# A graph layer on one core: zeros through TensorE in the first segment, PSUM operands for x and h, and another order at the end

## The chip, the core and the metric

The kernel runs on one core of one Trainium2 chip. A core has TensorE for matrix products (PE in the profile, its weight loads PEld), VectorE (DVE), ScalarE (ACT), GpSimd (POOL) and SyncE (SP). In this kernel SP issues nearly all plain DMAs and POOL issues the scatters. TensorE writes to PSUM, 8 banks of 512 fp32 values per partition. The metric is the device time of one launch in microseconds (us), as the median of several runs. "Granted clock" is the share of the full TensorE clock that the records show; in this trace it is 1.0 or 0.5 at any moment, and means lie between.

## The reference, cut to what matters

```
h = relu(layernorm(x)) @ W_in2f                 # 12500 nodes x 128
Wij = ssp(f_ij @ W_f1 + b_f1) @ W_f2 + b_f2     # 412500 edges, 20 -> 128 -> 128
Wij = Wij * rcut_ij[:, None]
x_ij = h[idx_j] * Wij                           # idx_j = dst, sorted
agg = segment_sum(x_ij, idx_i)                  # idx_i = src, unsorted
out = ssp(agg @ W_o1 + b_o1) @ W_o2 + b_o2
return x + out                                  # ssp(x) = softplus(x) - log 2
```

The edges come sorted by the node whose h they read, so that reading is local. The node they are summed into is in no order, so the messages have to be moved to their place.

## The kernel before

**Chunks and segments.** The edges are cut into 806 chunks of 512 edges, four chunks to a group. The chunks are split into seven segments of 88, 44, 30, 14, 14, 8 and 4 groups. Every segment has its own table in HBM (`slots`). A chunk's 512 messages are scattered by POOL into the table of its segment, each to a slot in the block of 128 nodes that it belongs to; four scatters of 128 rows to a chunk. When a segment is complete, its table is read back in "units" (`Collect`), and TensorE adds the rows to their nodes with a 0/1 matrix. So segment 1 is collected while the chunks of segment 2 and later ones are worked on, and during the chunks of the first segment there is no collecting at all. The first segment's chunks are 0 to 351; its collecting begins at step 359 (`DELAY` is 7).

**What one chunk takes.** TensorE: the filter layer `z` for a pair of chunks (`hidden`, L691, 20 rows x 512 columns, twice); the second filter layer `v` (`value`, L801, four products of 128 columns); the picking of the rows of h, `picked` (`pick`, L812, four products with a 0/1 matrix `at` that DVE makes at L785); two products for the ranks of the slots, `free` (L766, L733, 392 columns). ScalarE: softplus's parts of a pair (L700, L701, L703), the bias written into `v` (`bias`, L793), and `hg`, the picked rows times the cutoff (`picked`, L822). VectorE: `r` (L709), `top` (L738), `inb` (L714), and the message `o` = v * hg (`message`, L829 and L830). POOL: the four scatters of `o` (L834).

**The order of the work.** The order on every engine is written out by hand in `step(k, units)`, one call for every k: message of chunk k, then the end of the ranks (`top`) begun in the step before, then `keep` for sums that are finished, then `hg` and `v` of chunk k+1, the picking of chunk k+2, `at` of k+3, `r`, `inb`, the comparing of units (`compare`, L886, the 0/1 matrix `to`), ranks, softplus, the filter layer of the pair that begins at k+4, and last the adding of units on TensorE (`add`, L907). Engines take their instructions in this order. `picked` and `v` share three PSUM banks (tag `v`): the bank of `picked` of chunk k+2 comes free when the message of chunk k has been computed. `z` has a pair of banks of its own, free when `r` has read it. `behind` makes the first product of a filter layer, of `v` and of a picking wait also for a scatter eight steps back.

**Collecting.** `keep` copies (first segment, ScalarE, L928) or adds (later ones, VectorE, L930) a finished quad of four blocks from the PSUM bank `acc` to the sums `agg` in SBUF. There is one `acc` bank while chunks run. A planner spreads the units over the steps from the end of a segment up to step `NCH + BEYOND`; after a unit that ends a quad it lets no other unit into that step. The last segments are collected after the last chunk; then the output layer `finish` runs, quad by quad.

**h and x.** `make_h` computes h for a quad of 512 nodes, 25 quads in all, beside the chunks of the first segment (last at 1344 us). It keeps h as the sum of three bf16 parts: the first is a rounding of the PSUM tile `hps`, then `left` = hps - first part (L370), the second part a rounding of `left` (L371), the third `left` minus the second (L373). x is loaded again for the residual, for 14 quads early (`early_homes`, from step 300, bias added by VectorE at L426) and for the other quads after the last chunks (`late_homes`, bias added by POOL). `count_ps` holds 0 to 127 along the free axis in PSUM, for `inb` and `to`.

Of the kernel before, what the change touches and what calls it, by code (L numbers as in the profile page):

```python
# [17 lines left out]
P = 128  # L18
TG = 16
CH = 512  # L20
# [23 lines left out]
def gnn_kernel(  # L44
# [282 lines left out]
    def make_h(q, psum):  # L327

        n = min(QT, NTILE - q * QT)
        xb = early.pop(q, None)  # L330
        if xb is None:
            xb = load_x(q)
            for _ in range(3):
                yield
        st = ln.tile([P, QT, 6], F32, name="st")
        mv = ln.tile([P, QT, 2], F32, name="mv")
        for i in range(n):
            nc.vector.bn_stats(st[:, i, :], xb[:, i, :])
            nc.vector.bn_aggr(mv[:, i, :], st[:, i, :])

        rs = ln.tile([P, QT], F32, name="rs")
        nc.scalar.activation(rs[:, :n], mv[:, :n, 1], AF.Ln, bias=eps)
        nc.scalar.activation(rs[:, :n], rs[:, :n], AF.Exp, scale=-0.5)
        yield

        ve = ln.tile([P, QT], F32, name="ve")
        nc.vector.tensor_scalar(ve[:, :n], mv[:, :n, 1], EPS, -0.5, op0=ALU.add, op1=ALU.mult)
        r2 = ln.tile([P, QT], F32, name="r2")
        nc.vector.tensor_mul(r2[:, :n], rs[:, :n], rs[:, :n])
        nc.vector.tensor_mul(r2[:, :n], r2[:, :n], ve[:, :n])  # L350
        nc.vector.scalar_tensor_tensor(rs[:, :n], r2[:, :n], 1.5, rs[:, :n],
                                       op0=ALU.add, op1=ALU.mult)
        for i in range(n):
            nc.vector.tensor_scalar(xb[:, i, :], xb[:, i, :], mv[:, i, 0:1], rs[:, i:i + 1],
                                    op0=ALU.subtract, op1=ALU.mult)
        yield
        xps = psum.tile([P, QT, P], F32, name="xps", tag="acc")
        for i in range(n):
            nc.tensor.transpose(xps[:, i, :], xb[:, i, :], ident)
        xT = ln.tile([P, QT, P], F32, name="xT")  # L360
        nc.scalar.activation(xT[:, :n, :], xps[:, :n, :], AF.Relu)
        yield
        hps = psum.tile([P, QT, P], F32, name="hps", tag="acc")
        for i in range(n):
            nc.tensor.matmul(hps[:, i, :], xT[:, i, :], win, start=True, stop=True)
        hb = ln.tile([P, QT, 3, P], BF16, name="hb")
        nc.scalar.activation(hb[:, :n, 0, :], hps[:, :n, :], AF.Copy)
        yield
        left = ln.tile([P, QT, P], F32, name="left")
        nc.vector.tensor_sub(left[:, :n, :], hps[:, :n, :], hb[:, :n, 0, :])  # L370
        nc.scalar.activation(hb[:, :n, 1, :], left[:, :n, :], AF.Copy)  # L371
        yield
        nc.vector.tensor_sub(hb[:, :n, 2, :], left[:, :n, :], hb[:, :n, 1, :])  # L373
        for (b, rows), table in zip(tables, h3_t):
            lo = max(0, b - q * QN) // P
            hi = min(n, (b + rows - q * QN) // P)
            if lo < hi:
                r = q * QN + lo * P - b
                nc.sync.dma_start(
                    table[r:r + (hi - lo) * P, :].rearrange("(c p) f -> p c f", p=P),  # L380
                    hb[:, lo:hi, :, :].rearrange("p c k f -> p c (k f)"))
                if b + rows == QN:
                    yield
            if q == NQ - 1:
                for r in range(NTILE * P - b, rows, P):
                    if r >= 0:
                        nc.sync.dma_start(table[r:r + P, :], none)
        nc.sync.dma_start(
            h3[q * QN:q * QN + n * P, :].rearrange("(c p) f -> p c f", p=P),
            hb[:, :n, :, :].rearrange("p c k f -> p c (k f)"))  # L390
        yield
# [28 lines left out]
        for p, cs, rows in pieces:  # L420
            nc.sync.dma_start(xo[:p, cs, :], x[rows, :].rearrange("(c p) f -> p c f", p=p))

    def x_bias(xo, pieces, engine=nc.vector):
        for p, cs, rows in pieces:
            xi = xo[:p, cs, :]
            engine.tensor_add(xi, xi, spread(bo2[:p, :], xi.shape[1]))  # L426

    def finish(t0, n, sT, quad, psum, z, xo=None, bank=("v", 3)):

# [108 lines left out]
    with tc.tile_pool(name="edge", bufs=2) as edge, tc.tile_pool(  # L538
# [8 lines left out]
        free_v = free.rearrange("p (t b) -> p t b", b=NBLK)  # L547


        count_ps = state_ps.tile([P, P], F32, name="count_ps")  # L550

        def clear(seg):

            todo = []

            def put(b, e, low):

                half = seg.tiles(b) * P // 2
                v = seg.views[VIEWS][seg.row(b):seg.row(e), :].rearrange(
                    "(r c) f -> r (c f)", c=half)  # L560
                for q in range(0, 2 * (e - b), P):
                    n = min(P, 2 * (e - b) - q)
                    for r in range(low, half - low, ZN * ZR):
                        w = min(ZN * ZR, half - low - r)
                        todo.append((
                            v[q:q + n, r * RW:(r + w) * RW].rearrange("r (k f) -> r k f", f=ZR * RW),
                            zero[:n, None, :].to_broadcast([n, w // ZR, ZR * RW])))

            full = (NBLK - 1) // BG * BG
            for b, e in ((0, seg.b0), (seg.b0, min(seg.b1, full)), (seg.b1, full)):  # L570
                if b < e:
                    put(b, e, seg.low)

            for b in range(full, NBLK):
                low = seg.low if b < NBLK - 1 else seg.low_last
                half = seg.tiles(b) * P // 2
                n = (half - 2 * low) // ZR
                for r in range(2):
                    r0 = seg.row(b) + r * half + low
                    todo.append((seg.views[VIEWS][r0:r0 + n * ZR, :]  # L580
                                 .rearrange("(q c) f -> q (c f)", c=ZR), zero[:n, :]))
            return todo

        puts = []

# [8 lines left out]
        class Group:  # L594
# [91 lines left out]
            def hidden(self, c):  # L686

                z = psum.tile([P, 2, CH], F32, name="z")
                for k in range(2):
                    rows = slice(32 * (c + k), 32 * (c + k) + RBF)  # L690
                    mm = nc.tensor.matmul(z[:, k, :], wf1[rows, :], self.f[rows, :],  # L691
                                          start=True, stop=True)
                    if k == 0:
                        behind(mm, self.g * NCHUNK + c - LZ, 3)
                self.pair[c] = z
# [110 lines left out]

            def pick(self, c, at, ps):

                near = self.near.pop(c)
                k = self.g * NCHUNK + c - 2  # L810
                for i in range(QT):
                    mm = nc.tensor.matmul(ps[:, i, :], at[:, i * P:(i + 1) * P], near,  # L812
                                          start=i == 0, stop=i == QT - 1, skip_group_check=True)
                    if i == 0:
                        behind(mm, k, 2 + k % 2)
# [118 lines left out]
        groups = {}  # L934
        NEXT = table_of.index(1) - 1
        LG, LW, LR, LZ = 12, 6, 6, 4
        DELAY, BEYOND = 7, 14

        def of(k):
            return groups[k // NCHUNK], k % NCHUNK  # L940
# [52 lines left out]
        def step(k, units=()):  # L993
# [19 lines left out]
                for _ in r:  # L1013
                    pass
            tops.clear()
            for c in owed:
                c.keep()
            owed.clear()
            if has(k + 1):
                g, c = of(k + 1)  # L1020
                hgs[k + 1] = g.picked(c, ps.pop(k + 1))
# [10 lines left out]
            part("blocks", min(k + LR + 1, 2 * k + 3), blocks)  # L1032
            for c, u in units:
                c.compare(u)
            upto = max(made["rank"], min(k + LR, 2 * k + 3))
            ready = [ranks(j) for j in range(made["rank"] + 1, upto + 1)]
            made["rank"] = upto
# [63 lines left out]
                if todo[i - 1][1].ends(todo[i - 1][2]):  # L1101
                    break

        def x_ahead(homes, engine):

            pending = []
            for q, xo in homes:
# [5 lines left out]
                yield  # L1113
                yield
                if len(pending) > 2:
                    x_bias(*pending.pop(0), engine)
            for w in pending:
                yield
                x_bias(*w, engine)

        def as_quad(t):
            return t.rearrange("p (c f) -> p c f", f=P)

        xs = {}
        NX = 14

        def early_homes():
            for q in range(NX):
                if q < 6:
                    yield q, quad.tile([P, QT, P], F32, name="xo", bufs=6)  # L1130
                elif q < 12:
                    yield q, ln.tile([P, QT, P], F32, name="xo", tag=("xb", "xT", "left")[q // 2 - 3],
                                     bufs=2)
                else:
                    t = ln.tile([P, QT, 3, P], BF16, name="xo", tag="hb", bufs=2)
                    yield q, as_quad(t.rearrange("p c k f -> p (c k f)")[:, :2 * CH].bitcast(F32))
# [14 lines left out]
        def rest():  # L1151
# [14 lines left out]
                    yield  # L1166
            yield from ranges(psum)
            late_biases(psum)

        def side():  # L1170

# [11 lines left out]
        with tc.manual_schedule():  # L1183
# [27 lines left out]
            made["rank"] = 0  # L1211
            group(1)
            aside = side()
            x_early = x_ahead(early_homes(), nc.vector)
            x_late = x_ahead(late_homes(), nc.gpsimd)
            for k in range(-3, max(NCH, max(units) + 1)):
                for seg, d in zeros.get(k, ()):
                    seg.clears.append(nc.sync.dma_start(*d).ins.name)
# [122 lines left out]
```

## Time and profile before

| | |
|---|---|
| median of 8 runs | 5287.85 us (5268.48 to 5309.7) |
| the profiled execution, its own time | 5317.66 us |
| its span, first to last instruction | 5315.9 us |
| POOL: scatters L834 | 3224, 3099.0 us busy, 961 ns each |
| PE busy, share of the span | 3715.0 us, 70% |
| DVE, ACT busy | 3139.1 us, 2784.8 us |
| granted clock, 500 to 1000 us and 2500 to 3000 us | 0.66 and 0.83 |

The stages in time: chunk 0 is scattered at 23 us; the collecting of the first segment begins with `acc` sums near 2300 us (first L928 at 2302.9 us); the last scatter is at 5185.1 us; from there to about 5240 us units are loaded and added, and then the output layer runs to the end. Times per chunk are read off POOL, because every chunk has exactly four scatters: the number of L834 in a window divided by four is the number of chunks. "Releaser" is what ended an engine's wait; `remote` means that a semaphore changed for which the profile shows no instruction.

### The profile page before, as it was taken

How to read it: one execution, taken by the hardware profiler on the slowest of the kernel's cores; microseconds unless marked ns; L12 is line 12 of the kernel's file. 1: busy time of each engine (PE TensorE's matmuls, PEld its weight loads, DVE VectorE, ACT ScalarE, POOL GpSimd, SP SyncE). 2: the span in 40 equal slices, each digit the busy share in tenths (PEclk: the TensorE clock that was granted, in tenths of full speed). 3: DMA queues.
4: the chain of work that ended last, by engine and by line, in shares of the span. 5: the costliest groups of instructions: out<-in, count | busy, mean ns of one | idle time of the engine just before them, and what ended most of it. 6: DMA issues, size and time to landing. Idle time of an engine off the chain costs nothing. (4 is left out here: it accounts for less than half of the span.)

```text
span 5315.9 us, 74340 instructions
## 1 busy us (share of the span) xinstructions
PE 3715.0 (70%) x21594; PEld 2847.6 (54%) x21594; DVE 3139.1 (59%) x7101; ACT 2784.8 (52%) x5466; POOL 3136.7 (59%) x3292
## 2 busy tenths in 40 slices
PE   5565655556556555588887787787777777777778
PEld 3344433444334333366666666666666666665657
DVE  5555555555444444566666666566666666666667
ACT  5555555555555545555555555455544454554443
POOL 5666666666666666666665565555555555555552
PEclk7666666666666666688888888888888888888889
DMA  4445444444433334455656555566655665565546
GB/s 144 143 146 152 141 140 147 125 146 126 117 96 97 96 113 135 124 181 177 182 178 210 169 168 170 154 182 191 173 165 157 188 189 150 171 191 156 158 131 194
DMA packets 515221, 820.65 MB, mean 154 GB/s; under 512 B 177188, under 2 KB 312728, under 8 KB 514812
## 3 DMA queue, kind: packets, MB, share of 16 engines
q1 hardware_dynamic: 411212, 602.55, 40.2%
q0 software_dynamic: 103168, 213.15, 12.0%
q8 instruction: 180, 2.95, 0.2%
q14 instruction: 229, 1.88, 0.1%
q10 hardware_dynamic: 432, 0.13, 0.0%
HBM read 419.75 MB, written 395.69 MB: 153 GB/s over the span
## 5 line engine op out<-in xcount | busy, mean ns | idle before, releaser
L834 POOL DMA_INDIRECT slots<-o,slot x3224 | 3099.0, 961 | 2083.1 <-DVE o L830 1192.1
L822 ACT ACTIVATE hg<-picked,rcut 128x128 f32<-128x128 f32 x3224 | 912.3, 365 | 1371.0 <-remote 732.4
L907 PEld LDWEIGHTS acc<-to,m 128*128 128x128 f32 x8152 | 1202.4, 229 | 467.9 <-issue 307.7
L907 PE MATMUL acc<-to,m 128*128 128x128 f32 x8152 | 1296.7, 320 | 196.6 <-issue 99.5
L801 PEld LDWEIGHTS v<-wf,r 128*128 128x128 f32 x6448 | 1084.5, 249 | 446.6 <-issue 302.9
L801 PE MATMUL v<-wf,r 128*128 128x128 f32 x6448 | 1183.0, 338 | 174.3 <-issue 109.1
L830 DVE TENSOR_TENSOR o<-v,hg 128x512 f32<-128x512 f32 x806 | 552.6, 686 | 969.6 <-remote 513.4
L691 PE MATMUL z<-f,wf 20*128 20x512 f32 x1612 | 626.3, 854 | 468.3 <-DVE r L709 270.0
L886 DVE TENSOR_TENSOR to<-count_ps,m 128x640 f32<-128x640 f32 (+3 forms) x793 | 636.3, 826 | 251.6 <-remote 104.0
L738 DVE TENSOR_REDUCE top<-free 128x4 f32<-128x392 f32 x806 | 448.8, 557 | 475.3 <-remote 267.1
L793 ACT ACTIVATE v<-bf 128x512 f32<-128x512 f32 x806 | 486.0, 603 | 449.0 <-DVE o L830 243.9
L812 PE MATMUL picked<-near,at 96*128 96x128 bf16 x3224 | 386.2, 253 | 374.7 <-DVE o L830 259.5
L709 DVE SCALAR_TENSOR_TENSOR r<-z,nbf,a 128x1024 f32<-128x1024 f32 x403 | 514.0, 1275 | 101.3 <-ACT a L703 56.8
L766 PE MATMUL free<-inb,rest_of 128*128 128x392 f16 x806 | 327.8, 407 | 341.1 <-issue 214.5
L700 ACT ACTIVATE a<-z,bf 128x1024 f32<-128x1024 f32 x403 | 445.0, 1104 | 226.5 <-remote 126.2
L812 PEld LDWEIGHTS <-at 96*128 96x128 bf16 x3224 | 308.2, 116 | 432.8 <-issue 408.1
L691 PEld LDWEIGHTS z<-f,wf 20*128 20x128 f32 x1612 | 156.1, 233 | 679.5 <-DVE r L709 362.3
L703 ACT ACTIVATE a<-a,half 128x1024 f32<-128x1024 f32 x403 | 462.7, 1148 | 13.1
L714 DVE TENSOR_TENSOR inb<-count_ps,blk 128x392 f16<-128x392 f32 x806 | 445.5, 553 | 0.0
L701 ACT ACTIVATE a<-a 128x1024 f32<-128x1024 f32 x403 | 425.9, 1057 | 12.8
L733 PE MATMUL free<-inb,after 128*128 128x392 f16 x806 | 330.9, 411 | 7.1 <-DVE inb L714 3.8
L785 DVE TENSOR_SCALAR at<-rel,prow 96x512 bf16<-96x512 bf16 x806 | 283.3, 352 | 0.0
(113 smaller groups left out, 1226.2 us busy)
## 6 DMA issues: line engine op xcount, KB each, us to landing
m<-slots SPq DMA_DIRECT2D x307, 387.0 KB
m<-slots SPq DMA_DIRECT2D x278, 322.5 KB
rel<-rel_d SPq DMA_DIRECT2D x202, 384.0 KB
slots<-o,slot POOLq DMA_INDIRECT x3224
m<-slots SPq DMA_DIRECT2D x193, 258.0 KB
slots<-zero SPq DMA_DIRECT2D x96, 387.0 KB
f<-in_f_t SPq DMA_DIRECT2D x404, 80.0 KB
slots<-zero SPq DMA_DIRECT2D x58, 516.0 KB
```

The lines of the kernel that those rows point to most:

```text
L691: mm = nc.tensor.matmul(z[:, k, :], wf1[rows, :], self.f[rows, :], start=True, stop=True)
L703: nc.scalar.activation(a, a, AF.Ln, bias=half, scale=0.5)
L709: nc.vector.scalar_tensor_tensor(r, z, nbf1, a, op0=ALU.max, op1=ALU.add)
L738: nc.vector.tensor_reduce(self.top[:, c * QT:(c + 1) * QT], free_v, axis=mybir.AxisListType.X, op=ALU.max)
L793: nc.scalar.activation(v, spread(bf12, QT), AF.Copy)
L801: mm = nc.tensor.matmul(v[:, i, :], r[:, i * P:(i + 1) * P], wf2, start=False, stop=True, skip_group_check=True)
L812: mm = nc.tensor.matmul(ps[:, i, :], at[:, i * P:(i + 1) * P], near, start=i == 0, stop=i == QT - 1, skip_group_check=True)
L822: nc.scalar.activation(hg[:, i, :], ps[:, i, :], AF.Copy, scale=self.rcut[:, j:j + 1])
L830: nc.vector.tensor_mul(o[:, :, :P], v, hg)
L834: put = nc.gpsimd.indirect_dma_start(out=views[j % VIEWS], out_offset=bass.IndirectOffsetOnAxis(ap=self.slot[:, j:j + 1], axis=0), in_=o[: ...
L886: nc.vector.tensor_tensor(to[:, :n, :], count_ps[:, None, :].to_broadcast([P, n, P]), m[:, :n, P:].to_broadcast([P, n, P]), op=ALU.is_equal)
L907: nc.tensor.matmul(self.acc[b // QT][:, i, :], m[:, j, :P], to[:, j, :], start=t == 0, stop=t == self.seg.tiles(b) - 1)
```

## The change

There are four parts.

1. In the steps of the first segment (chunks 8 to 358) TensorE multiplies zeros: 12 products of 384 columns into the bank of `z` in front of each pair's filter layer, and 6 into the bank of `picked` in front of each picking. The results are overwritten by the products that follow. These are 4218 products, and as many weight loads.
2. `keep` moves in `step`, but only in the steps after the last chunk (k >= `NCH`) that have units: there a finished quad is added after the first `compare` of the step and no longer before it. In all other steps, so while chunks run, it stays where it was.
3. PSUM operands: `left` is gone, the differences are formed in the PSUM tile `hps` itself. The bias bo2 is copied to PSUM beside `count_ps`, and the early bias addition of x reads it there. With the room that this frees, two more quads of x are loaded early (16, before 14) and two fewer at the end.
4. `BEYOND`, the number of steps after the last chunk over which the planner may spread units, is 8 (before 14).

```diff
-        left = ln.tile([P, QT, P], F32, name="left")
-        nc.vector.tensor_sub(left[:, :n, :], hps[:, :n, :], hb[:, :n, 0, :])
-        nc.scalar.activation(hb[:, :n, 1, :], left[:, :n, :], AF.Copy)
+        nc.vector.tensor_sub(hps[:, :n, :], hps[:, :n, :], hb[:, :n, 0, :])
+        nc.scalar.activation(hb[:, :n, 1, :], hps[:, :n, :], AF.Copy)
         yield
-        nc.vector.tensor_sub(hb[:, :n, 2, :], left[:, :n, :], hb[:, :n, 1, :])
+        nc.vector.tensor_sub(hb[:, :n, 2, :], hps[:, :n, :], hb[:, :n, 1, :])
...
-    def x_bias(xo, pieces, engine=nc.vector):
+    def x_bias(xo, pieces, engine=nc.vector, b=bo2):
...
-        count_ps = state_ps.tile([P, P], F32, name="count_ps")
+        numbers = state_ps.tile([P, CH], F32, name="numbers")
+        count_ps, bo2_ps = numbers[:, :P], numbers[:, P:2 * P]
...
+        def idle(bank, n):
+
+            for _ in range(n):
+                nc.tensor.matmul(bank[:, :3 * P], none[:, :P], none, start=True, stop=True,
+                                 skip_group_check=True)
...
                 z = psum.tile([P, 2, CH], F32, name="z")
+                if 8 <= self.g * NCHUNK + c < segs[1].c0 + DELAY:
+                    idle(z[:, 0, :], 12)
                 for k in range(2):
...
             def pick(self, c, at, ps):
 
+                if 8 <= self.g * NCHUNK + c < segs[1].c0 + DELAY:
+                    idle(ps.rearrange("p t f -> p (t f)"), 6)
                 near = self.near.pop(c)
...
-        DELAY, BEYOND = 7, 14
+        DELAY, BEYOND = 7, 8
...
-            for c in owed:
-                c.keep()
-            owed.clear()
+            def keep():
+                for c in owed:
+                    c.keep()
+                owed.clear()
+
+            if k < NCH or not units:
+                keep()
...
             for c, u in units:
                 c.compare(u)
+                keep()
...
-        NX = 14
+        NX = 16
...
             late_biases(psum)
+            nc.scalar.activation(bo2_ps, bo2, AF.Copy)
...
-            x_early = x_ahead(early_homes(), nc.vector)
-            x_late = x_ahead(late_homes(), nc.gpsimd)
+            x_early = x_ahead(early_homes(), nc.vector, bo2_ps)
+            x_late = x_ahead(late_homes(), nc.gpsimd, bo2)
```

`none` is a bf16 tile of zeros that both kernels have, for rows of the tables that no node owns.

## The prediction

> **What bounds the kernel now.** I read the page first: busy shares, the 40 slices, and the costliest group.
>
> ```profile
> span 5315.9 us, 74340 instructions
> PE   5565655556556555588887787787777777777778
> POOL 5666666666666666666665565555555555555552
> PEclk7666666666666666688888888888888888888889
> ...
> L834 POOL DMA_INDIRECT slots<-o,slot x3224 | 3099.0, 961 | 2083.1 <-DVE o L830 1192.1
> ```
>
> No engine is full in any slice before the end. The scatters come nearest: four to a chunk, 961 ns each and 0.30 us between two of them, so 4 x 1.26 = 5.05 us is the least that a chunk can take. The first 17 slices have a clock of 0.6, the later ones 0.8. Next the table of stretches: three of the first stage, one where segment 1 is collected, and the end of the collecting.
>
> ```profile
> core 0: us, PE busy (x) PEld busy (x) DVE busy (x) ACT busy (x) POOL busy (x), PEclk, DMA share, GB/s
> 500.00:1000.00 500.00, 297.34 (x1415) 202.44 (x1413) 274.46 (x725) 285.42 (x572) 313.26 (x325) 0.66 0.48 142
> 1500.00:2000.00 500.00, 288.54 (x1290) 193.09 (x1289) 235.34 (x562) 269.26 (x529) 311.70 (x324) 0.63 0.37 103
> 2500.00:3000.00 500.00, 408.32 (x2612) 328.65 (x2611) 319.57 (x659) 266.14 (x523) 302.48 (x316) 0.83 0.62 187
> ...
> 5187.00:5235.00 48.00, 38.56 (x305) 35.13 (x304) 35.48 (x57) 0.00 (x0) 12.62 (x12) 1.00 0.93 267
> ```
>
> POOL's instructions divided by four are chunks: 500 / 81.25 = 6.15 us per chunk in the first row, 6.17 in the next, 500 / 79 = 6.33 in the third. From the first to the second DVE falls by 39 us and the DMA share by 0.11, and the pace stays: neither sets it. What lies above 5.05 us is waiting, so the waits of 150 to 2150 us come next (us in total, times, longest).
>
> ```profile
> POOL slots L834 <- DVE o L830: 389.2, 116, 6.7
> ...
> ACT hg L822 <- remote: 309.0, 70, 10.8
> ...
> DVE o L830 <- remote: 261.8, 55, 11.0
> PE picked L812 <- DVE o L830: 213.9, 57, 9.9
> ```
>
> Once in every 18 us or so all wait at once. The timeline shows one such place (start, duration, instruction, idle time before it and its releaser).
>
> ```profile
> 1258.22 2.08 PE L801 MATMUL v<-wf,r 128*128 128x128 f32 x8 [0.15 <-issue]
> ...
> 1262.39 0.96 POOL L834 DMA_INDIRECT slots<-o,slot  x1 [0.30 <-issue]
> 1265.64 1.14 ACT L822 ACTIVATE hg<-picked,rcut 128x128 f32<-128x128 f32 x4 [4.17 <-remote]
> 1265.66 0.69 DVE L830 TENSOR_TENSOR o<-v,hg 128x512 f32<-128x512 f32 x1 [5.95 <-remote]
> ...
> 1266.40 0.59 PE L812 MATMUL picked<-near,at 96*128 96x128 bf16 x4 [6.10 <-DVE o L830]
> ...
> 1266.62 0.96 POOL L834 DMA_INDIRECT slots<-o,slot  x1 [3.28 <-DVE o L830]
> ```
>
> POOL scatters what it has, twelve scatters or three chunks, and runs dry at 1263.35. PE's products for the next chunks ended at 1260.30 by the records, but `hg` and `o` are released only at 1265.64, by a semaphore for which no instruction shows. Then the message takes 0.69 us, and POOL goes on after a pause of 3.28. Counted over the scatters from 150 to 2150 us: 113 runs, 80 of them of 12 scatters, with pauses of 3.42 us on average. From 2450 to 5000: 205 runs, 161 of 8 scatters, pauses of 3.07. So two things set the pace: the length of a run and of a pause.
>
> What holds the release back I can't read from the trace. But the pause goes with the clock. Where the clock between two runs has a mean under 0.75, pauses have a mean of 3.51 us in the first stage (103 of 112) and 3.63 in the second (74 of 205); where it is above, 2.37 (9) and 2.74 (131).
>
> The profiled execution took 5317.7 us, 29.8 above the median of 5287.85; I sum against its time and take 29.8 off at the end.
>
> **The change part by part. (1) Zeros.** The written order of PE after the change differs from before by 4218 products and their weight loads and by nothing else: 6 ahead of each of 351 pickings, 12 ahead of each of 176 filter layers, 12 per chunk. The first of each six or twelve takes over the wait for its bank (`picked` for the message two chunks back, `z` for `r`), so it can't run before that wait ends, and what it delays is the picking, the ranks, `z` and the next chunk's `v`, all behind it on PE. Price: two products of 392 columns start 0.17 us apart at the full clock (1205.46, 1205.63) and 0.33 at half (1203.46, 1203.79), so 12 take 2.0 or 4.0 us; their weights load beside them (0.10 to 0.15 each). PE's own work for one chunk, from the timeline of 1199 to 1214 us, is v 1.16, picked 0.39, two free 0.50 and half of a pair's z 0.57, together 2.62 at full clock; at half 2.08, 0.63, 0.86 and 1.04, together 4.61. With zeros 4.6 or 8.6, against 6.15 us per chunk. At full clock it fits and delays nothing for long; at half it doesn't, and POOL lives on the finished messages.
>
> Gain: with zeros PE issues 16 + 12 instructions a chunk, near the 33 of the third row (2612 / 79), where 36% of the pauses (74 of 205) are cold, not 92% (103 of 112). So 56% of the pauses turn warm. A warm pause is shorter by 0.89 us by the second stage's means and by 1.14 by the first's; I take 1.0. 351 x 6.15 = 2160 us hold 122 pauses: 122 x 0.56 x 1.0 = 68 us less.
> Bounds: a gain up to 159, if runs also grow from 12 scatters to 16 (a pause over four chunks and not three: 3.12 x (1/3 - 1/4) = 0.26 x 351 = 91 more); a loss up to 235, if the zeros cut the runs to the 8 of the second stage and the clock stays cold (6.82 us a chunk in that stage's cold cycles: 0.67 x 351). I take the gain, as the row with the high clock has the shorter pause in both stages.
>
> The Trainium skill speaks against it ("TensorE: Matmul & The Clock Gate", Part 1): the clock is gated by a free-running window of about 3.4 us; one idle window halves it and a busy one restores it. The 6.10 us that PE stands still above must then hold an idle window nearly always, and the zeros, which wait for the same message, can't fill them. By that rule every pause stays cold and part 1 saves nothing; the sum would be 5283. In the second stage, with pauses about as long, 64% stay warm, so I go by the rows.
>
> **(2) The order at the end.** `keep` moves only after the last chunk, in the 18 or so steps whose units are added there, about 5187 to 5235 us. The waits of that stretch:
>
> ```profile
> DVE agg L930 <- PE acc L907: 12.7, 19, 1.1
> PEld acc L907 <- DVE to L886: 11.3, 17, 0.8
> ...
> PE acc L907 <- DVE to L886: 8.1, 17, 0.6
> ```
>
> A quad takes 2.54 us: `agg` 0.69, two `to` 1.28, and 0.65 in which DVE waits for PE's last product, while PE then waits 0.49 for `to`. With `agg` between the two `to`, PE's product ends beside the first one. The most to be gained is the 12.7 us. But the DMA share of this stretch is 0.93 at 267 GB/s: the units' loads (SP, in order) can quicken by 7% of 48 us, 3.4 us. Two x loads of 256 KB leave it: 0.52 MB / 267 GB/s = 2.0. Together -5; bounds 0 and -12.7 - 2.0.
>
> **(3) The rest, at nothing.** `left` in PSUM: 25 quads; 0.691 us where one operand is in PSUM, 0.679 where none is, so under 0.6 us in all, on a DVE that is 50% busy. The bank of `hps` stays taken until L373 instead of L370, 7 us later (1337.4, 1344.4); the next quad uses it some 50 us on. Bound +-2, should a quad's end delay a message. Two more early x: two loads on SP and 2 x 0.68 on DVE from step 300 on, and one copy of about 0.2 us on ACT; POOL loses 2 x 1.27 at the end, where it waits for x. Covers: POOL's pauses, which these engines also sit out; uncovered, under 2 us. `BEYOND` moves no instruction: the units end at the same step with 8.
>
> Sum: 5317.7 - 68 - 5 = 5245; less 29.8: 5215 us.
>
> **The rivals.**
> *Longer runs (0.12).* A warm PE gets further ahead before each hold, and runs grow to 16. For: 13 of the 113 runs have 16. Against: the banks (two pickings ahead) don't grow. 5215 - 91 = 5124.
> *Shorter runs: slower (0.33).* Zeros lie in PE's order as unit products do in the second stage. There the clock is high, and yet a chunk takes longer (6.33 against 6.15) as runs have 8 scatters, not 12. Place: `v` of the next chunk, behind up to 18 zeros, 3 us at full clock and 6 at half. It decides once PE needs more than 6.15 us a chunk, that is when over about 40% of its time stays cold ((6.15 - 4.6) / 4.0). Price by the row: 0.18 x 351 = +63; 5317.7 + 63 - 5 - 29.8 = 5346, and up to 5518 if cold too. Against: without zeros DVE and DMA also had less to do in the first stage.
> *The hold ends with POOL's last scatter, whatever the clock (0.12).* In the timeline the release comes 2.3 us after POOL ran dry. If pauses stay at 3.4 and the zeros only fill PE's idle time: 5317.7 - 5 - 29.8 = 5283, no change.
>
> **How the numbers follow.** Forecast 0.43, its own range 5195 to 5262 (a saving of 0.3 to 1.3 of the 68, the end's bounds added); longer runs 0.12; no effect 0.12; shorter runs 0.33. A measurement of this kernel tells about 0.3%, 16 us, from none. Faster: 0.43 + 0.12 = 0.55; same 0.12; slower 0.33. For the range I leave out half of the longer runs (below 5120) and a third of the shorter ones' worse half (above 5400): 5120 to 5400.
>
> **What would show it.** Right: the clock of 500 to 2000 us above 0.8; L834's count per 500 us up from 325 to about 335; runs still of 12 scatters, pauses near 2.8; the waits of `hg` for `remote` down by a third. At the end, DVE's waits before `agg` near nothing and the DMA share at 1. Wrong: runs of 8 scatters in the first stage, `v` waiting for PE's queue and `o` for `v`; or a clock that stays at 0.65 because the zeros fall outside the hold.

## The result, and the profile after

The changed kernel takes 5371.14 us (median of 17 runs, 5354.77 to 5411.11) against 5289.13 for the kernel before (46 runs): a ratio of 1.0164, with a 95% interval of 1.0147 to 1.018. The forecast was 5215; the time lies inside the stated range, but on the other side of no change, where the rival of shorter runs had put 5346. The profiled execution of after took 5408.2 us, 37 above its median, and that of before 29 above the 5289, so the two traces can be laid side by side.

The page of after: span, the clock in 40 slices, the scatters and the zeros in front of the pickings.

```profile
span 5406.4 us, 82293 instructions
...
PEclk8888888888888888888888888888788887788889
...
L844 POOL DMA_INDIRECT slots<-o,slot x3224 | 3102.3, 962 | 2171.9 <-DVE o L840 1292.1
...
L587 PE MATMUL picked<-none 128*128 128x384 bf16 x2106 | 456.3, 354 | 161.1 <-DVE o L840 100.4
```

The clock did what the forecast said, 0.6 became 0.8 in the first slices, but POOL waits for the message longer than before (1292.1 us, 1192.1 before). The same stretches as before:

```profile
core 0: us, PE busy (x) PEld busy (x) DVE busy (x) ACT busy (x) POOL busy (x), PEclk, DMA share, GB/s
...
500.00:1000.00 500.00, 399.37 (x2313) 245.74 (x2310) 265.74 (x692) 275.85 (x552) 302.40 (x315) 0.88 0.45 137
...
1500.00:2000.00 500.00, 375.61 (x2215) 227.75 (x2213) 223.06 (x530) 267.17 (x520) 304.37 (x317) 0.88 0.35 97
...
2500.00:3000.00 500.00, 410.64 (x2631) 329.95 (x2630) 317.96 (x647) 268.99 (x530) 307.40 (x320) 0.83 0.62 188
```

At a clock of 0.88 in place of 0.66 and 0.63, POOL does 315 and 317 instructions where it did 325 and 324; the third row, behind the zeros, is as before. By the first scatter of each chunk: from chunk 8 to 358 it takes 2250.7 us (2165.8 before), from 358 to 800 2911.1 (2911.8), from 800 to the end 168.6 (164.7), up to chunk 8 76.0 (73.7). So 85 of the 90 us between the two traces lie where the zeros are. The waits of 150 to 2150 us (in total, times, longest):

```profile
POOL slots L844 <- DVE o L840: 463.1, 165, 7.2
PEld L587 <- issue: 405.9, 824, 5.7
...
ACT hg L832 <- remote: 203.4, 43, 10.8
DVE o L840 <- remote: 168.8, 46, 7.4
```

The waits for `remote` fell by a third, as forecast, and nothing came of it: POOL stops more often. Counted over the scatters of 150 to 2250 us there are 160 runs, 81 of 8 scatters and 42 of 12 (before, in 100 us less: 113 runs, 80 of 12), with pauses of 2.96 us on average (3.42). Runs of 8 in the first stage were the forecast's own sign of being wrong. The pauses are shorter, but there are so many more that the sum grows: in 150 to 2150 us 153 pauses take 451 us, before 113 took 388.

Where the time goes inside a pause, the timeline of after shows better than that of before did, as PE now has work left in it. TensorE alone, start, duration and idle time before it:

```profile
1238.49 0.22 PE L822 MATMUL picked<-near,at 96*128 96x128 bf16 x1
1239.82 0.22 PE L822 MATMUL picked<-near,at 96*128 96x128 bf16 x1 [1.11 <-issue]
1240.56 0.22 PE L822 MATMUL picked<-near,at 96*128 96x128 bf16 x1 [0.52 <-issue]
1241.96 0.22 PE L822 MATMUL picked<-near,at 96*128 96x128 bf16 x1 [1.19 <-issue]
1242.67 0.49 PE L774 MATMUL free<-inb,rest_of 128*128 128x392 f16 x1 [0.49 <-issue]
```

Four products that take 0.39 us together elsewhere take 3.7. Between two of them stand 0.7 or 1.4 us, and the weight loads between them start 1.4 us apart: PE gets one instruction every 0.7 us and waits for nothing else that the profile shows. In the first stage of the kernel before I had seen the same 0.7 us only on SP. I call such a stretch a hold from here on.

### The profile page after: what moved, and what is told of

The parts are those of the page before. It is cut to its first block, busy times and chain, and to the rows that moved or that the text cites. A ratio compares the mean times of both kernels' runs of the same rounds, so it can differ in the third digit from the quotient of the medians.

```text
span 5406.4 us, 82293 instructions
## 1 busy us (share of the span) xinstructions
PE 4183.4 (77%) x25812; PEld 3046.5 (56%) x25812; DVE 3140.2 (58%) x7103; ACT 2791.7 (52%) x5467; POOL 3137.6 (58%) x3290
## 5 line engine op out<-in xcount | busy, mean ns | idle before, releaser
L844 POOL DMA_INDIRECT slots<-o,slot x3224 | 3102.3, 962 | 2171.9 <-DVE o L840 1292.1
L809 PE MATMUL v<-wf,r 128*128 128x128 f32 x6448 | 1010.9, 300 | 124.6 <-issue 113.0
L809 PEld LDWEIGHTS v<-wf,r 128*128 128x128 f32 x6448 | 908.3, 212 | 327.8 <-issue 269.5
L587 PEld LDWEIGHTS <-none 128*128 128x128 bf16 x4218 | 449.9, 107 | 649.1 <-issue 466.2
L896 DVE TENSOR_TENSOR to<-numbers,m 128x640 f32<-128x640 f32 (+3 forms) x793 | 637.7, 827 | 278.9 <-PE acc L917 90.0
L699 PE MATMUL z<-f,wf 20*128 20x512 f32 x1612 | 546.6, 742 | 257.0 <-DVE r L717 192.4
L587 PE MATMUL picked<-none 128*128 128x384 bf16 x2106 | 456.3, 354 | 161.1 <-DVE o L840 100.4
L587 PE MATMUL z<-none 128*128 128x384 bf16 x2112 | 447.1, 370 | 122.4 <-DVE r L717 69.8
L722 DVE TENSOR_TENSOR inb<-numbers,blk 128x392 f16<-128x392 f32 x806 | 445.6, 553 | 0.0
L774 PE MATMUL free<-inb,rest_of 128*128 128x392 f16 x806 | 297.3, 369 | 187.0 <-DVE top L746 102.4
L822 PE MATMUL picked<-near,at 96*128 96x128 bf16 x3224 | 353.7, 233 | 103.3 <-issue 58.4
```

The costliest lines, as they stand in the source:

```text
L587: nc.tensor.matmul(bank[:, :3 * P], none[:, :P], none, start=True, stop=True, skip_group_check=True)
L809: mm = nc.tensor.matmul(v[:, i, :], r[:, i * P:(i + 1) * P], wf2, start=False, stop=True, skip_group_check=True)
L844: put = nc.gpsimd.indirect_dma_start(out=views[j % VIEWS], out_offset=bass.IndirectOffsetOnAxis(ap=self.slot[:, j:j + 1], axis=0), in_=o[: ...
L896: nc.vector.tensor_tensor(to[:, :n, :], count_ps[:, None, :].to_broadcast([P, n, P]), m[:, :n, P:].to_broadcast([P, n, P]), op=ALU.is_equal)
```

## The experiments

The kernel was run on several chips, and they are of two kinds. On some the kernel before takes 5289 to 5367 us and shows the holds; on others it takes 4226 to 4228 us and shows none. The trace tells the kinds apart: of SP's FUSED_REGOPS, MOVE and SEQ_ASSERT in 150 to 2150 us, 251 of 1300 last over 0.5 us in the first trace of before, and 0 of 1592 on a chip without holds. One chip number came up once as the one and once as the other kind, so I can't say that it is the chip; "chip" below stands for the one that a series ran on, in the state that it then had. A percentage is against the kernel before on the same chip in the same series.

**First series (holds; before 5366.58).** Two theories: PE's time in its order, or the number of instructions. First the other parts of the change without any zeros:

```
-            for _ in range(n):
+            for _ in range(0):
```

> All parts of the change but the zeros. Two theories of the loss. A, PE's order: the zeros' time (2.0 us a chunk at full clock) lies in front of the next `v`, and POOL runs dry sooner. B, the count: all engines are held once in some 200 instructions, whichever engine they run on; from one pause of POOL to the next there are 197 instructions (17.6 us) in the first stage before, 199 (12.4 us) in the second, 186 (13.0 us) in the first stage after. Both say here: the other parts are worth 0 to -15, so 5275 to 5290, pauses and runs of the first stage as before.

Measured 5368.54, ratio 1.0009 (0.999 to 1.0027). The other parts are worth nothing that can be measured here; the zeros are the loss. Next as many zeros without work:

```
-                nc.tensor.matmul(bank[:, :3 * P], none[:, :P], none, start=True, stop=True,
+                nc.tensor.matmul(bank[:1, :1], none[:, :1], none[:, :1], start=True, stop=True,
```

> As many zero products and weight loads in the same places, each of 1 weight column and 1 moving column, so almost no work for the array. A: no PE time to speak of, so 5280 to 5300, runs of 12 scatters as before. B: 8436 instructions more are 8436 / 197 = 43 pauses more, of 3.4 us as the clock stays low: +146, so 5400 to 5450.

Measured 5416.38, 1.0085 (1.0054 to 1.0115). This is the run that takes the forecast's main step apart. Its stretch from 500 to 1000 us:

```profile
500.00:1000.00 500.00, 347.73 (x2234) 235.46 (x2234) 253.84 (x659) 266.33 (x533) 295.79 (x308) 0.62 0.45 136
```

The clock is low (0.62) and stays low, PE's order is longer by only 0.4 us a chunk (six of these products take 0.22 us, twelve 0.37), and POOL does 308. The runs are 98 of 8 scatters and 26 of 12, and the pauses have a mean of 2.96 us, the same as after the whole change at 0.88. So the pauses can become shorter without a high clock. PE's order (A: 5280 to 5300, at most 11 us above the kernel before) doesn't explain the loss either. The number does: theory B said 43 pauses more, and in 150 to 2150 us there are 158 where e1 has 119. Its price (+146) was three times too high, because the pauses were shorter too: together they take 466 us, in e1 425.

Then the time without the number, and half of both:

```
-            for _ in range(n):
-                nc.tensor.matmul(bank[:, :3 * P], none[:, :P], none, start=True, stop=True,
+            for _ in range(n // 6):
+                nc.tensor.matmul(bank, zero[:, :P], zero[:, :CH], start=True, stop=True,
```

> As much PE time in few products: one fp32 product of 512 columns in front of each picking, two in front of each pair's filter layer (703 products, about 1.16 us each at full clock, 2.3 us a chunk against 2.0). A: as after or worse, 5370 to 5390. B: 703 products are 2812 instructions with their loads (fp32 takes two records each), 14 pauses more x 3.0 = +43, and shorter pauses from the higher clock 122 x 0.46 = -56: 5260 to 5290, runs of nearly 12.

```
-            for _ in range(n):
+            for _ in range(n // 2):
```

> Half of the zeros: 3 in front of each picking, 6 in front of each filter layer, 384 columns each. A: 1.0 us a chunk at full clock, little of it on the path: 5290 to 5315. B: 4218 instructions more, 21 pauses x 3.2 = +68, some 20 to 50 of it back by shorter pauses: 5310 to 5340.

Measured 5399.9, 1.0063 (1.0039 to 1.0088), and 5378.2, 1.0034 (1.0016 to 1.0053). The few long ones keep the clock at 0.85 and PE busy nearly as long as the change does (380 of the 500 us from 500 on, 399 with the change), and cost less than the tiny ones: a third of the instructions, two thirds of the loss. At e2's price, 50 us for 8436 instructions, they would cost 17 us; they cost 33 (21 to 47), so the number is not the whole of it, and PE's time seems to count as well. Half the zeros cost least of all. Over the first stage of the profiles (chunk 8 to 358): 2207.3 without zeros, 2212.9 half, 2220.8 few long, 2249.3 tiny. The profiled execution without zeros stood 24 us above its median and that with half of them 29 below, so the small ones of these differences tell little.

**Second series (no holds; before 4227.91).** The whole change again, the tiny zeros twice over (the first diff, on the kernel of e2), `hg` in one instruction in place of four, without zeros (the second), and the zeros of the filter layer alone (the third):

> The changed kernel again, beside the runs that follow, since another chip's time of the kernel before differs (5367 against 5289). Ratio to before as on the first chip, 1.015 to 1.018, with 160 pauses or so in 150 to 2150 us. From the runs so far (tiny zeros +50, 8436 instructions, 0.4 us of PE's order per chunk; half +12; few long ones +33, 2812 instructions, 2.4 us) I work out, as cost per instruction and per us of PE's order: 8436 instructions at 5.5 ns = 46, and 2.2 us x 351 at 2 to 4% = 15 to 30: +60 to +80.

```
-            for _ in range(n):
+            for _ in range(2 * n):
```

> The tiny zeros twice over, 12 in front of each picking and 24 in front of each filter layer: 16872 instructions more than without zeros. A, PE's order: 0.8 us a chunk in place of 0.4, of which the first 0.4 cost nearly nothing: 0 to +20 over the tiny zeros. B, the count: as much again, +90 to +110 over the kernel before, with runs of 8 and 4 scatters.

```
-                for i in range(QT):
-                    j = c * QT + i
-                    nc.scalar.activation(hg[:, i, :], ps[:, i, :], AF.Copy,
-                                         scale=self.rcut[:, j:j + 1])
+                nc.vector.tensor_mul(hg, ps, self.rcut[:, c * QT:(c + 1) * QT, None]
+                                     .to_broadcast([P, QT, P]))
```

> No zeros, and `hg` formed by one VectorE product with the cutoff spread over the columns in place of four ScalarE copies: 3 x 806 = 2418 instructions fewer on all stages, none of them on TensorE; ScalarE is relieved of 1.46 us a chunk and VectorE gets 0.69 more. If the count holds for every engine, at 5.5 to 15 ns each: -13 to -36 against the kernel before. If only PE's instructions count, or if VectorE's order is the limit: 0 to +40.

```
             def pick(self, c, at, ps):
-                if 8 <= self.g * NCHUNK + c < segs[1].c0 + DELAY:
-                    idle(ps.rearrange("p t f -> p (t f)"), 6)
```

> Only the 12 zeros in front of each pair's filter layer (2112 products, 4224 instructions with loads), none in front of the pickings. Half of the count and of the PE time of the whole change. By the count half of its loss, +25 to +40; if the zeros of the pickings alone cost, because they stand in front of what the next message needs, 0 to +10.

Measured: 4214.81, 0.9974 (0.9965 to 0.9984) for the whole change; 4214.91, 0.9971 (0.996 to 0.9982) for the tiny zeros twice; 4314.77, 1.0208 (1.0191 to 1.0226) for `hg`; 4214.69, 0.9974 (0.9965 to 0.9984) for the filter layer's alone. No expectation held, because the holds were gone. The whole change on this chip:

```profile
500.00:1000.00 500.00, 436.43 (x2907) 282.47 (x2906) 328.68 (x862) 347.00 (x695) 379.67 (x396) 0.97 0.57 170
```

396 scatters in 500 us are 5.05 us a chunk, which is POOL's floor in the forecast; it holds from 500 to 4000 us, with zeros and behind them. Zeros of any of these kinds cost nothing, because POOL never waits for a message. What remains is the same 13 us gain in all three, which the zeros can't have made: e15 and e17 below have none and gain 11 to 13 us as well. The kernel with one `hg` instruction lost its time after chunk 358 (2316.5 us to chunk 800 where the others take 2235 to 2240), where VectorE also compares the units:

```profile
ACT v L801 <- DVE hg L830: 996.2, 283, 9.3
...
POOL slots L842 <- DVE o L838: 66.8, 81, 5.4
```

In 2000 to 4000 us ScalarE's `v` waits 996 us for VectorE's `hg`, as `v` and `picked` share their PSUM banks, and POOL waits 67 us for the message.

**Third series (holds; before 5297.84).** Four of these again, now side by side:

> The chip of the last runs had no holds: POOL went through at 5.05 us a chunk (396 scatters in 500 us), the kernel before took 4228 us, and zeros of any kind cost nothing there. So the loss belongs to the holds. On a chip with holds (before at 5250 to 5400): the whole change +1.3 to +1.8%, and now beside the same chip's other three. On a chip without (before near 4230): -0.2 to -0.4% as in the last runs.

> All parts but the zeros. With holds: as before within 0.2%, as on the first such chip. Without holds: the -13 us of the whole change are the end's and x's, so -0.2 to -0.4% as well; if the zeros had a share in the gain, less than -0.2%.

> The doubled tiny zeros, 16872 instructions more, 0.8 us a chunk in PE's order. With holds: the count of all instructions says +1.7 to +2.1% (twice the +0.85% of the tiny ones); PE's order says +0.9 to +1.2%. Without holds: -0.3% as in the last runs.

> `hg` in one VectorE instruction, 2418 instructions of ScalarE and their pauses fewer. With holds: if every engine's instructions count, -0.2 to -0.6%; if only PE's, 0 to +0.8%. Without holds: +2% as in the last runs, where VectorE became the limit in the later stages.

| zeros | instructions more | median us, ratio (interval) | chunk 8 to 358, us | mean, median pause, us | clock 500 to 1000 |
|---|---|---|---|---|---|
| none (e10) | 0 | 5298.62, 0.9995 (0.9976 to 1.0014) | 2160.5 | 3.32, 3.25 | 0.65 |
| whole change (e9) | 8436 | 5381.46, 1.0172 (1.0138 to 1.0206) | 2237.8 | 2.94, 2.64 | 0.87 |
| tiny, twice (e11) | 16872 | 5469.03, 1.0329 (1.0299 to 1.036) | 2335.7 | 3.47, 2.83 | 0.65 |
| none, one `hg` (e12) | -2418 | 5307.39, 1.0012 (0.9983 to 1.004) | 2170.2 | 3.58, 3.14 | 0.64 |

The tiny zeros twice over take about 0.8 us a chunk of PE's order, the change's zeros 2.2 at full clock by the durations of their rows; they lose 175 and 77 us in the first stage. That is 10.4 and 9.2 ns an instruction: twice the instructions lose twice as much, with far less of PE's time and a low clock. So the number decides here. That PE's time counts for nothing is not shown (e3 speaks against it). The timeline of TensorE in e11 shows how:

```profile
1211.62 0.36 PE L587 MATMUL z<-none 128*1 128x1 bf16 x9 [0.54 <-issue]
1212.51 0.16 PE L587 MATMUL z<-none 128*1 128x1 bf16 x1 [0.53 <-issue]
1213.92 0.19 PE L587 MATMUL z<-none 128*1 128x1 bf16 x2 [1.25 <-issue]
1214.63 0.16 PE L587 MATMUL z<-none 128*1 128x1 bf16 x1 [0.52 <-issue]
1215.37 0.21 PE L587 MATMUL z<-none 128*1 128x1 bf16 x3 [0.57 <-issue]
1216.03 0.16 PE L587 MATMUL z<-none 128*1 128x1 bf16 x1 [0.45 <-issue]
...
1218.34 3.36 PE L699 MATMUL z<-f,wf 20*128 20x512 f32 x4
...
1230.67 0.74 PE L587 MATMUL z<-none 128*1 128x1 bf16 x24 [2.31 <-DVE r L717]
1231.34 1.13 PE L699 MATMUL z<-f,wf 20*128 20x512 f32 x4
```

Outside a hold the 24 products start within 0.67 us (1230.67 to 1231.34). Caught by a hold they took 6.7 (1211.62 to 1218.34), in steps of 0.7, and the filter layer stood behind them. I counted the steps from one start on PE to the next, weight loads included, that last 0.6 to 0.8 or 1.25 to 1.45 us in 150 to 2150 us, one or two such instructions: 39 without zeros, 188 and 228 with the change's, 602 with the tiny ones twice over. On chips without holds the same zeros leave 55 and 56. The one `hg` instruction is within the noise here, which doesn't tell whether ScalarE's instructions count, as VectorE got more to do.

**Fourth and fifth series (no holds; before 4225.85 and 4227.39).** To separate number and time further, and to add instructions on ScalarE alone; both series met chips without holds, so they answer another question.

> The tiny zeros again, now to be compared with the whole change's +1.7% at the same number of instructions (8436). On a chip with holds: if only the number counts, +1.5 to +1.7%, as the whole change (9.2 ns each by the last two runs of it, 10.4 by the doubled tiny ones); if PE's time counts too, less than that, near the +0.85% of the first run of it. Without holds: -0.3%.

The doubled zeros of the change:

```
-            for _ in range(n):
+            for _ in range(2 * n):
```

> Twice the zeros of the change: 12 in front of each picking, 24 in front of each filter layer, 384 columns, 16872 instructions more, 4.1 us a chunk at full clock on top of PE's own 2.6. With holds: by the count alone as the doubled tiny ones, +3.1 to +3.5%; if PE's order counts, PE then needs 6.7 us a chunk and more, and the loss is +5% or more. Without holds PE's 6.7 us against POOL's 5.05 make 350 x 1.65 = 580 us, +13%.

```
-                for i in range(QT):
-                    j = c * QT + i
-                    nc.scalar.activation(hg[:, i, :], ps[:, i, :], AF.Copy,
+                for i in range(2 * QT):
+                    j = c * QT + i // 2
+                    f = slice(i % 2 * 64, i % 2 * 64 + 64)
+                    nc.scalar.activation(hg[:, i // 2, f], ps[:, i // 2, f], AF.Copy,
                                          scale=self.rcut[:, j:j + 1])
```

> No zeros; `hg` in eight ScalarE instructions of 64 columns in place of four of 128: 4 x 806 = 3224 instructions more, all on ScalarE, on all stages, at about 1 us more of ScalarE per chunk. With holds: at the 10 ns of the zeros +32 us, +0.5 to +0.7%, if instructions of every engine count; 0 to +0.2% if only TensorE's do. Without holds: -0.3%, unless ScalarE becomes late.

> The few long zeros again, 2812 instructions with the PE time of the change (2.4 us a chunk), clock 0.85. With holds: by the count alone 28 us, +0.5%; if PE's time counts, +1.2% or more. Without holds: -0.3%, as PE's 5.0 us a chunk just fit.

> The last runs were again on a chip without holds, where eight `hg` instructions cost nothing. On a chip with holds: 3224 instructions more on ScalarE alone. If instructions of every engine count, +0.5 to +0.7%; if only TensorE's, within 0.2% of before.

> The tiny zeros on a chip with holds: +0.85% as on the first such chip, or up to +1.7% if the number alone counts. Without holds: -0.25%, as in the last runs.

Measured: tiny 4213.55, 0.9975 (0.9965 to 0.9984); eight `hg` 4214.74, 0.9973 (0.9964 to 0.9983); few long 4214.91, 0.9975 (0.9965 to 0.9986); and again eight `hg` 4214.33, 0.9971 (0.9958 to 0.9983), tiny 4214.42, 0.9968 (0.9957 to 0.9979). All as the whole change there, -11 to -13 us. Only the doubled zeros fall out: 4573.87, 1.0824 (1.0806 to 1.0842).

```profile
500.00:1000.00 500.00, 499.14 (x3369) 324.06 (x3367) 277.53 (x730) 288.72 (x577) 311.70 (x326) 1.00 0.47 142
```

Here PE is busy 499 of 500 us at a clock of 1.00, and a chunk takes 6.08 us (2128.2 us for 350): without holds, PE's time in its order becomes a loss only when PE is full. I had expected 6.7 us a chunk; the sum of row durations was 10% too high (in the rows shown above a product's start lies before the end of the one ahead of it).

## Why the prediction was wrong, point by point

**The step that failed is the 68 us of gain**, 122 pauses x 0.56 x 1.0 us, with "a warm pause is shorter by 0.89 us by the second stage's means and by 1.14 by the first's; I take 1.0". More pauses did turn warm: 60 of 152 are cold after the change, 103 of 112 before, so the count of 56% was nearly met (92% to 39%). The pauses also became shorter, by 0.46 us on average where the sum took 0.56. But their number, which the sum left as it was, rose from 113 to 153 in the same 2000 us, and that outweighed it.

The shorter pauses are not the clock's work either. e2 has a mean pause of 2.96 us at a clock of 0.62, e4 2.97 at 0.77, e3 2.96 at 0.85, the change 2.96 at 0.88; without zeros it is 3.32 (e10) and 3.57 (e1). What these four share is runs of 8 scatters beside those of 12, and a pause goes with the run ahead of it: in 150 to 2150 us of before its mean is 2.20 us behind a run of 8 (8 pauses) and 3.51 behind one of 12 (80), after the change 2.76 (77) and 4.36 (39), in e2 2.52 (98) and 4.95 (26). The run is not all: e11 has mostly runs of 8 and a mean of 3.47. In the trace of before, warm pauses lay mostly in the second stage with its runs of 8, and of the few in the first stage seven stood behind runs of 8 and two behind runs of 12.

The forecast also took the clock over the pause itself. Taken over the 3 us ahead of the pause it makes no difference: in the first stage of before, behind runs of 12, 3.51 us cold (52) and 3.52 warm (28); in the second stage 3.05 cold (47) and 3.07 warm (158). Over 2 us it is 3.54 and 3.44 in the first stage, over 5 us 3.40 and 3.63. So cause and effect most likely stood the wrong way round: PE stands still in a long pause, and the mean clock of that pause is low because it is long.

**The other term of the sum was missing**: what a PE instruction costs in a hold. I priced the zeros at the 0.17 and 0.33 us of the fastest and the slowest rows of PE, and took "PE's products for the next chunks ended at 1260.30 by the records" to mean that PE had nothing left to do in a pause. The 0.7 us steps stood in the trace of before on SP, and in the second stage on PE (385 such steps in 2500 to 5000 us); I took them for something beside the matter. How the added instructions become added pauses can be counted: from one pause of POOL to the next there are 198 instructions of all engines in the first stage of before and 186 after the change, while the time between pauses falls from 17.6 to 13.0 us. Of the 43, 14 and 21 more pauses that theory B gave e2, e3 and e4, 39, 28 and 24 came. In e11 it breaks: by the same rate 16872 instructions are 86 pauses more, 37 came, and the pauses were longer.

One slip in the sums bears on nothing: the forecast's own range of 5195 to 5262 takes 5 us for the end at both ends; with the end's bounds added, as it says, it is 5185 to 5267.

**The rule set against the change.** The rule of the clock gate ("TensorE: Matmul & The Clock Gate", Part 1, in the Trainium skill) was weighed as the one that spoke against the change, with no gain from part 1. The rows disagree with that use of it: the clock rose to 0.88 although pauses remained. They agree with its sum in so far as there was no gain, but for another reason.

**The slower rival** had the sign, the shorter runs and nearly the size: +63 us, 85 measured between the two traces and 77 in e9 against e10. Its cause was not right: it was to decide once PE needs over 6.15 us a chunk, and PE was busy 399.37 us for 78.75 chunks, 5.07. The tiny zeros twice over (e11) need far less time and lose more. That its price came near was in part luck: it was read off the second stage, which has nearly as many PE products a chunk (33 against 28) and the same holds, but for another reason. e14 shows what the rival's own mechanism looks like.

**Longer runs** and **no effect** were wrong: runs became shorter, and the pauses changed.

**The order at the end** was priced at -5, between 0 and -14.7. Its mechanism is there. e10 from 5175 to 5217 us:

```profile
5175.00:5217.00 42.00, 38.40 (x311) 35.88 (x311) 36.53 (x58) 0.00 (x0) 10.05 (x10) 1.00 0.99 296
```

and its waits from 5173 us on:

```profile
POOL xr L425 <- DMA xr<-in_x: 16.9, 6, 4.2
...
DVE to L896 <- DMA m<-slots: 3.1, 9, 0.6
...
DVE agg L940 <- PE acc L917: 1.3, 2, 0.7
```

DVE no longer waits for PE's last product in each quad (12.7 us before, here 1.3, in the changed kernel's own trace 3.0); it waits for units, and the DMA share is 0.99 (0.93 before), as forecast. e10 is the best of four, though: the change's own trace has a share of 0.93 from 5280 to 5325 us, and from the last scatter to the first product of the output layer it takes 46.7 us in e10, but 51.9 in after, 52.0 in e9 and 52.9 in e1, before 53.5. In the medians with holds nothing of it can be told from none (0.9995 and 1.0009, with intervals of 10 us to either side that hold the 5 us too); without holds every kernel with these parts gains 11 to 13 us, unless PE or VectorE became the limit. I put that gain down to the end and to x together, but no run undid one of them alone, so how it divides is open.

**The rest, at nothing** (`left` in PSUM, x, `BEYOND`): chunk 8 to 358 takes 2160.5 us in e10 and 2165.8 in before. That agrees, as far as single traces of two series can tell; no run undid one of these parts alone.

**What stays open.** What makes the holds, and why some series have them and others not. The loads of instructions, which the trace shows as DMA packets of kind `instruction`, show no tie to them: one begins in the 8 us ahead of a pause for 40% of the pauses of before's first stage and for 41% of instants taken at random (47% and 47% after the change), and e5 without holds has more such packets (197 from 150 to 2150 us, 129 before). A rival that no run tests: every execution here comes with a span and a clock of its own, so it was recorded while it ran, and a cost that goes by the number of instructions is also what recording could make; no run here is without it. Whether instructions of ScalarE or VectorE count as PE's do is not known either: e15 and e17 were made for that and met no holds. And the size per instruction is open: 9 to 10 ns in the third series, but by the medians of the first series, where the whole change was not run, 6 for the tiny zeros, 3 for the half and 12 for the few long ones.

## What to carry to other kernels

A wait on something that the profile doesn't name need not be a wait that belongs to the kernel: before building a gain on it, look whether plain instructions (here SP's, at 0.7 us) are slow in the same places, and price what is added by what an instruction costs there. A difference between two groups of pauses is no effect of the clock while the groups also differ in what comes before the pause, and a clock averaged over a pause is partly made by the pause; a variant that adds the instructions without the work tells it in one run. Work added to keep an engine warm pays only where that engine's time decides; without the holds POOL's 5.05 us a chunk did, and zeros were free up to the point where PE was full.

## What was unexpected of the hardware

The kernel before took 4228 us in one series and 5289 in another, and the changed one 4215 and 5371, with the same work in it (in the changed kernel's two traces POOL is busy 3138.8 and 3137.6 us, DVE 3151.9 and 3140.2): the kernel had been read as bound by waits between engines, and where the holds are absent it is bound by POOL up to the last scatters. In a hold PE and SP get one instruction in about 0.7 us, so a product of one column costs about as much as one of 384 (10.4 and 9.2 ns each, averaged over the first stage, in e11 and e9). And the clock of TensorE rose from 0.65 to 0.87 without any time gained.
